# A graph-convolution and expert kernel: edge rows, statistics and the first projection in another order at the start

## The chip, the cores and the metric

The kernel runs on one core of a Trainium2 chip. The metric is the device time of one execution in microseconds (us), the median of three runs. One further execution was taken with the hardware profiler; its own time stands beside its span below. Engines: PE is TensorE, DVE VectorE, ACT ScalarE, POOL GpSimd, SP SyncE.

## The reference, cut to what matters

Two layers on 625 rows of 1024 features: a relational graph convolution with 20,000 edges and two relations, and a layer of eight experts (two taken per row) with two shared ones. The change touches the start of the first layer only:

```python
h      = layernorm(x)                            # 625 x 1024
norm_x = ln_weight * h * rsqrt(mean(h*h) + 1e-6)
out    = norm_x @ W_root + bias                  # 1024 -> 286
for r in range(2):
    w    = (edge_type == r)
    msg  = norm_x[src] @ W_rel[r] * w[:, None]
    sums = segment_sum(msg, dst, 625)
    cnt  = segment_sum(w, dst, 625)
    out  = out + sums / maximum(cnt, 1)[:, None]
x = x + h + elu(out) @ wo
x = x + experts(layernorm(x))
```

The edges come sorted by dst.

## The kernel before, in words

The 625 rows are five tiles of 125, called row 0 to row 4 here. The graph layer is done without gathers. The kernel counts, for each pair (source row, destination and relation), how many edges there are, and multiplies the projected rows with these counts.

**Loads (L520 to L552).** SP issues edge types, sources, x's row 0, the root weights, x's rows 1, then 2 and 3 in one load, row 4, and both relation weights (`load_x`, `load_w`), in this order; ACT issues the destinations and the layer-norm weights. POOL issues the bias (`cb`, L610), small vectors and the router's weights on a queue of its own.

**Edge columns (`edge_columns`, L664).** The three edge lists arrive as rows of 250. DVE turns them into float rows (L667 to L672), PE transposes them (L677), and ACT and DVE make three columns of them (L687 to L695): the source's position within its tile, a value that names the tile as a power of 16, and the destination key.

**Statistics (`stats`, L753).** For a row: two `bn_stats` on DVE, one for each half of 512, the aggregate, the negated mean (L760), and h = x - mean on ACT (L765). `scales` (L771) makes the factors of both norms from the variance.

**To columns (`to_columns`, L789).** PE transposes h in two groups of four blocks (L795); ACT evicts the first group in four instructions that multiply by the weights (L801), DVE the second in one (L798).

**Counts (`count_windows`, L828).** The edges are taken in 160 columns of 125, in groups of 4 (four groups) and then 8 (eighteen groups). For a group, DVE makes a one-hot of the sources (L849), multiplies it by the tile's value (L850), and a one-hot of the destination keys (L852). PE then does one count for each column (L868; two where a window crosses an accumulator's end).

**Projections (`project`, L886).** Projection i is eight steps of PE for one row and one weight matrix (L891): the first five are the root weights on rows 0 to 4, then the relations. Each step shows as two matmuls in the profile, about 0.51 us together.

**Order.** Below the loop stands an order written by hand: `at(c, f, ...)` runs f after the count of column c (L987 to L1021). A scheduler that knows estimated durations then orders each engine's instructions; `tc.issue_after(x)` keeps an instruction behind x on its engine, and each engine works in its order. Before the loop stand warm-up matmuls (`warm`, L970), the edge columns and the statistics of row 0; the first projection follows the count of column 7.

Of the kernel before, what the change touches and what calls it, by code (L numbers as in the profile page):

```python
# [18 lines left out]
D = 1024  # L19
E = 20000  # L20
R = 2
# [4 lines left out]
TP = 125  # L26
NT = N // TP
KD = D // 128
EP = 125
EC = E // EP  # L30
# [8 lines left out]
SPAN = (EP - 1 + 2 * SLACK) // DEG + 2  # L39
GROUPS = (4,) * 4 + (8,) * 18  # L40
# [412 lines left out]
def sparse_kernel(  # L453
# [24 lines left out]
    nc = tc.nc  # L478
# [33 lines left out]
    fbig = pool(front, "fbig", side="right")  # L512
    oneh = pool(front, "oneh", 8, side="right")
# [28 lines left out]
    def load_w(r, w):  # L542
        nc.sync.dma_start(wg[:, :, r, :], w.rearrange("(k p) f -> p k f", p=128))

    load_x(0, 1)
    load_w(R, W_root)
    load_x(1, 1)
    load_x(2, 2)
    for r in PARTS:
# [114 lines left out]
    def edge_columns():  # L664
        rowf = fbig.tile([EH, 2, 2 * EP], F32, name="rowf")
        two = [EH, 2, EP]
        nc.vector.tensor_tensor(rowf[:, 0].rearrange("c (j p) -> c j p", j=2),  # L667
                                rows_i["ety"].rearrange("c (j p) -> c j p", j=2),
                                low[:, 1][:, :, None].to_broadcast(two), op=ALU.subtract)
        nc.vector.scalar_tensor_tensor(rowf[:, 1], rows_i["dst"], float(R), rowf[:, 0],  # L670
                                       op0=ALU.mult, op1=ALU.add)
        nc.vector.tensor_copy(rowf[:, 0], rows_i["src"])  # L672
        p = ps_mm("p_edge")
        pv = p[:EP, : 2 * EC].rearrange("p (a j c) -> p a j c", a=2, j=2)
        for a in (0, 1):
            for j in range(2):
                nc.tensor.transpose(pv[:, a, j, :], rowf[:, a, j * EP : (j + 1) * EP], ident[:EH, :EH])  # L677
        wide = [EP, EH, 2, 2]

        def column(v):  # L680
            return v.rearrange("p (c j) b -> p c j b", j=2)

        def pairs(v):
            return v.rearrange("p j c -> p c j")[:, :, :, None].to_broadcast(wide)

        with tc.issue_after(table.ins):
            nc.scalar.copy(column(cols[:, KW_]), pairs(pv[:, 1]))  # L687

        q = fbig.tile([EP, 3, 2, EH], F32, name="q")
        nc.vector.tensor_scalar(q[:, 0], pv[:, 0], -float(TP // 2), 1.0 / TP, op0=ALU.add, op1=ALU.mult)  # L690
        nc.vector.tensor_scalar(q[:, 1], q[:, 0], ROUND, -ROUND, op0=ALU.add, op1=ALU.add)
        nc.vector.scalar_tensor_tensor(q[:, 2], q[:, 1], -float(TP), pv[:, 0], op0=ALU.mult, op1=ALU.add)
        nc.scalar.copy(column(cols[:, SP_]), pairs(q[:, 2]))

        return nc.vector.tensor_scalar(column(cols[:, VV_].bitcast(I16)), pairs(q[:, 1]), 4096.0, 7168.0,  # L695
                                       op0=ALU.mult, op1=ALU.add)


    flagf = const.tile([1, 2], F32, name="flagf")
# [53 lines left out]
    def stats(t):  # L753
        st = small.tile([TP, 2, 6], F32, tag="st", name=f"st_{t}")
        for s in range(2):
            with tc.issue_after((second[0] if t > 1 else evicted[1] if t else behind).ins):
                nc.vector.bn_stats(st[:, s, :], xh[:TP, t, s * 512 : (s + 1) * 512])
        nc.vector.bn_aggr(mv[:, t, :], st.rearrange("p a b -> p (a b)"))
        neg = small.tile([TP, 1], F32, tag="neg", name=f"neg_{t}")
        last = nc.vector.tensor_scalar(neg, mv[:, t, 0:1], -1.0, None, op0=ALU.mult)  # L760
        h = rows.tile([TP, D], F32, tag="h", name=f"h_{t}")
        with ExitStack() as order:
            if t == 1:
                order.enter_context(tc.issue_after(evicted[0].ins))
            moved = nc.scalar.activation(h, xh[:TP, t, :], AF.Identity, bias=neg)  # L765
        if t == 1:
            second.extend((last, moved))
        hs[t] = h
        return last
# [55 lines left out]
    MAXG = max(GROUPS)  # L825
    ends = [R * TP * min(DB * (b + 1), NT) for b in range((NT + DB - 1) // DB)]

    def count_windows(between):  # L828
        accs = []
        c0 = 0  # L830
        for g in GROUPS:
            oh_s = oneh.tile([EP, MAXG, 128], F16, tag="oh_s", name=f"ohs_{c0}")
            oh_k = oneh.tile([EP, MAXG, KR], F16, tag="oh_k", name=f"ohk_{c0}")

            def both(what, n):
                return [EP, g, n // 2, 2], cols[:, what, c0 : c0 + g][:, :, None, :].to_broadcast([EP, g, n // 2, 2])

            def halves(v):
                return v.rearrange("p g (a b) -> p g a b", b=2)

            order = ExitStack()
            if c0 == 0:
                order.enter_context(tc.issue_after(ahead.ins))
            elif c0 == 8:
                order.enter_context(tc.issue_after(second[0].ins))
            row = iota[:EP].rearrange("p (a b) -> p a b", b=2)
            shape, key = both(SP_, 128)
            os = halves(oh_s[:, :g, :])
            nc.vector.tensor_tensor(os, row[:, None].to_broadcast(shape), key, op=ALU.is_equal)  # L849
            nc.vector.tensor_tensor(os, os, both(VV_, 128)[1], op=ALU.mult)  # L850
            shape, key = both(KW_, KR)
            nc.vector.tensor_tensor(halves(oh_k[:, :g, :]), row[:, None, :SPAN].to_broadcast(shape), key,  # L852
                                    op=ALU.is_equal)
            order.close()
            for i in range(g):
                c = c0 + i
                a, z = R * LOW[c], R * min(LOW[c] + SPAN, N)
                for b, end in enumerate(ends):
                    base = ends[b - 1] if b else 0
                    f, t = max(a, base), min(z, end)  # L860
                    if f >= t:
                        continue
                    first = b == len(accs)
                    if first:
                        accs.append(psum[0].tile([128, 512], F32, tag="cnt", name=f"cnt_{b}", bufs=2))
                        nc.tensor.matmul(accs[b], nil[:, :128], nil, start=True, stop=False)
                    last = c == EC - 1 or R * LOW[c + 1] >= end
                    nc.tensor.matmul(accs[b][:, f - base : t - base], oh_s[:, i, :], oh_k[:, i, f - a : t - a],  # L868
                                     start=False, stop=last)
# [100 lines left out]
    def warm(n):  # L970
        for _ in range(n):
            nc.tensor.matmul(scrap[:, :128], iota, iota, start=True, stop=True)  # L972

    scrap = ps_acc("scrap")
    warm(24)
    behind = edge_columns()
    transpose_lnw()
    warm(40)
    ahead = stats(0)


# [541 lines left out]
```

## Time and profile before

| what | us |
|---|---|
| median of 3 runs | 304.88 (304.16 to 305.06) |
| profiled execution | 303.7 |
| its span | 301.4 |
| row 0's statistics begin on DVE | 7.68 |
| first count on PE | 10.30 |
| first transposes of x | 10.62 |
| first projection | 11.81 |
| last one-hot begins on DVE | 71.53 |
| end of the counts on PE | 73.08 |

A line of the timeline has the start, the busy time, the engine, the source line, the operation, what is written and read, the shape and the number of instructions merged. The chain of waits is followed back from the end; a piece of it has start, duration and what ran. In the parts with 40 characters, each is a fortieth of the span (7.5 us), in tenths of busy time.

### The profile page before, as it was taken

To read this page: it belongs to the slowest core of one execution; us is meant where nothing else is said; L and a number is where in the kernel's file an instruction comes from. 1 tells how busy PE (TensorE), PEld (TensorE's weight loads), DVE (VectorE), ACT (ScalarE), POOL (GpSimd) and SP (SyncE) were. 2 spreads that over 40 slices of the span, in tenths; PEclk is the share of its full clock that TensorE was granted. 3 is DMA by queue.
4 is the path that set the end of the run, shared out by engine and by line. 5 is a ranking of instruction groups with operands and counts; after the bars stand their busy time and mean duration, and the time that the engine had idled before them with its cause. 6 is when DMAs were issued, how large, how long until landed. Compare 5 with 4: busy or idle time off the path is not lost.

```text
span 301.4 us, 4682 instructions
## 1 busy us (share of the span) xinstructions
PE 290.8 (96%) x1649; PEld 194.9 (65%) x1649; DVE 168.4 (56%) x465; ACT 107.5 (36%) x246; POOL 45.2 (15%) x98
## 2 busy tenths in 40 slices
PE   8799999999999799999999999999999999999993
PEld 6687777787889534376777887887843334444452
DVE  5999999998327668756883122212223211255921
ACT  2455118355334432155123244638359311000000
POOL 9500000000000014240131212210003222200000
PEclk9999999999999999999999999999999999999998
DMA  7999910000009999965999253340057555479442
GB/s 243 304 318 393 421 65 2 0 2 1 0 17 340 348 348 391 400 195 182 348 396 410 86 203 96 114 141 3 0 190 276 221 209 210 191 291 385 161 138 73
DMA packets 27408, 61.15 MB, mean 203 GB/s; under 512 B 2176, under 2 KB 16007, under 8 KB 27375
## 3 DMA queue, kind: packets, MB, share of 16 engines
q1 hardware_dynamic: 21806, 43.77, 40.7%
q0 software_dynamic: 5280, 16.69, 15.7%
q10 hardware_dynamic: 294, 0.35, 0.5%
q8 instruction: 15, 0.25, 0.3%
q14 instruction: 13, 0.10, 0.1%
HBM read 42.76 MB, written 18.81 MB: 204 GB/s over the span
## 4 chain that ended last, share of the span: by engine, by line
PE 93%; DVE 4%; ACT 1%; issue 0%; ACTq 0%
PE p_pr L891 20%; PE p_h L1359 13%; PE p_yj L1417 13%; PE p_o L1472 11%; PE p_sh L1137 10%; PE p_y L952 6%; PE p_agg L909 6%; PE p_x L1340 3%; PE p_t L795 3%; PE cnt L868 2%; PE p_y L956 2%; PE p_hT L1371 1%; PE scrap L972 1%; PE p_gate L1085 1%; PE p_o L1474 1%; DVE ln_4s L727 0%
## 5 line engine op out<-in xcount | busy, mean ns | idle before, releaser
L891 PE MATMUL p_pr<-wg,nT 128*125 128x286 f32 x240 | 62.5, 409 | 0.0
L891 PEld LDWEIGHTS p_pr<-wg,nT 128*125 128x125 f32 x240 | 43.2, 187 | 11.3 <-ACT nT L801 0.2
L1359 PE MATMUL p_h<-w1a,xsT 128*128 (+2 forms) x176 | 40.0, 380 | 0.0
L1417 PE MATMUL p_yj<-w2a,hjT 128*128 (+2 forms) x88 | 38.6, 594 | 0.0
L1472 PE MATMUL p_o<-sw,shT 128*125 128x512 f32 (+1 forms) x88 | 36.1, 553 | 0.0
L1137 PE MATMUL p_sh<-h2T,sw 128*128 128x313 f32 (+1 forms) x128 | 35.2, 428 | 0.0
L1359 PEld LDWEIGHTS p_h<-w1a,xsT 128*128 128x128 f32 (+2 forms) x176 | 28.7, 168 | 7.4 <-issue 0.5
L1137 PEld LDWEIGHTS p_sh<-h2T,sw 128*128 128x128 f32 x128 | 23.6, 189 | 8.6 <-issue 0.2
L1417 PEld LDWEIGHTS p_yj<-w2a,hjT 128*128 128x128 f32 (+2 forms) x88 | 14.4, 168 | 22.4 <-issue 22.4
L1472 PEld LDWEIGHTS p_o<-sw,shT 128*125 128x125 f32 x88 | 16.4, 187 | 16.9 <-issue 16.2
L1421 DVE COPY ys<-p_yj 128x512 f32<-128x512 f32 x15 | 10.4, 692 | 28.7 <-PE p_yj L1417 26.5
L1363 DVE COPY hj<-p_h 128x256 f32<-128x256 f32 x11 | 4.7, 425 | 30.8 <-PE p_h L1359 30.8
L909 PE MATMUL p_agg<-P,CT 125*125 125x287 bf16 x150 | 20.1, 287 | 1.6 <-DVE agg L915 1.6
L966 POOL DMA_DIRECT2D x1d<-xh x10 | 5.3, 532 | 98.5 <-DVE xh L959 98.5
L909 PEld LDWEIGHTS <-CT 125*125 125x125 bf16 x150 | 18.5, 136 | 2.5 <-issue 2.0
L1425 POOL DMA_INDIRECT yt<-ys,row x11 | 10.8, 984 | 50.5 <-DVE ys L1421 50.5
L952 PE MATMUL p_y<-wo_t,eT 128*125 128x512 f32 x40 | 18.1, 595 | 0.0
L1332 POOL DMA_INDIRECT xs<-h2d,tok x11 | 11.2, 1015 | 45.0 <-PE p_x L1340 30.9
L1374 ACT ACTIVATE hjT<-p_hT,vT 128x128 f32<-128x128 f32 (+2 forms) x34 | 8.7, 332 | 24.5 <-PE p_hT L1371 24.5
L1344 DVE COPY xsT<-p_x 128x512 f32<-128x512 f32 x11 | 7.6, 692 | 17.4 <-PE p_x L1340 13.8
L1448 DVE SCALAR_TENSOR_TENSOR x<-p_o,x 125x512 f32<-125x512 f32 (+1 forms) x11 | 6.9, 641 | 16.3 <-PE p_o L1474 16.3
L1359 PE MATMUL p_h<-w1m,xsT 128*64 128x256 f32 (+1 forms) x96 | 14.7, 381 | 0.0
(302 smaller groups left out, 424.0 us busy)
## 6 DMA issues: line engine op xcount, KB each, us to landing
w1a<-in_L_ffn_W_dram SPq DMA_DIRECT2D x8, 1024.0 KB, 10.5
w2a<-in_L_ffn_W_dram SPq DMA_DIRECT2D x8, 1024.0 KB, 4.8
yt<-zero SPq DMA_DIRECT2D x2, 2560.0 KB
g<-yt SPq DMA_DIRECT2D x10, 512.0 KB, 6.7
sw<-in_L_ffn_sW_dram SPq DMA_DIRECT2D x4, 1024.0 KB, 5.0
x<-x1d SPq DMA_DIRECT2D x5, 500.0 KB
wg<-in_L_gnn_W_rel_dram SPq DMA_DIRECT2D x2, 1144.0 KB, 19.1
x1d<-xh POOLq DMA_DIRECT2D x5, 448.0 KB, 6.7
```

The lines of the kernel that those rows point to most:

```text
L795: nc.tensor.transpose(pv[:, k, :], row[:, at : at + 128], ident[:TP, :TP])
L891: nc.tensor.matmul(p[:TP, :F], nT[:, k, m * TP : (m + 1) * TP], wg[:, k, r, :], start=(k == 0), stop=(k == KD - 1))
L909: nc.tensor.matmul(p[:TP, : F + 1], CT[:, m, at : at + TP], P[:, m, r, i], start=(m == 0 and i == 0), stop=(m == NT - 1 and i == 2))
L952: nc.tensor.matmul(ps[s][:TP, :], eT[:, k, :], wo_t[:, k, s * 512 : (s + 1) * 512], start=(k == 0), stop=False)
L1137: nc.tensor.matmul(p[:, : z - a], sw1[:, i, k, t * 128 : (t + 1) * 128], h2T[:, k, a:z], start=(k == 0), stop=(k == KD - 1))
L1332: nc.gpsimd.indirect_dma_start(out=xs, out_offset=None, in_=h2d, in_offset=bass.IndirectOffsetOnAxis(ap=tok[:, j : j + 1], axis=0))
L1340: nc.tensor.transpose(p[:, k * 128 : (k + 1) * 128], xs[:, at : at + 128], ident)
L1359: nc.tensor.matmul(p[a:b, :H], xsT[j][:, k, a:b], w1m[j, a][:, 0, k, :] if a else w1a[:, bass.ds(e, 1), k, :], start=(k == 0), stop=(k == ...
L1417: made = nc.tensor.matmul(p[a:b], hjT[:, j, k, a:b], w2m[j, a, k][:, at] if a else w2a[:, bass.ds(e, 1), k, at], start=(k == 0), stop=(k = ...
L1421: nc.vector.tensor_copy(y[:, at], p)
L1425: sent.append(nc.gpsimd.indirect_dma_start(out=yt, out_offset=bass.IndirectOffsetOnAxis(ap=row[:, j : j + 1], axis=0), in_=y, in_offset=No ...
L1472: nc.tensor.matmul(p[:TP, :n], shT[:, i, k, own], sw2[:, i, k, at], start=(i == 0 and k == 0), stop=False)
```

## The change

- x's row 0 is loaded in two halves of 512 columns, and the root weights in two loads of four blocks each.
- In `edge_columns` the two transposes go to two PSUM tiles; the part that makes the source columns becomes `source_columns` and runs on DVE behind row 0's statistics. The position's column is written by DVE directly, where ACT copied it before (L693).
- h of rows 0 and 1 is made half by ACT and half by DVE.
- Row 0's transposes and the first projection are put ahead of all counts; the first group of one-hots is made behind row 0's eviction, and row 1's statistics behind these.
- Warm-up matmuls: 18 and 24 where there were 24 and 40.
- The hand-written places of statistics, transposes, scales and projections among the counts are moved.

```diff
-    load_x(0, 1)
-    load_w(R, W_root)
+    HALVES = [slice(s * 512, (s + 1) * 512) for s in range(2)]
+    for s in HALVES:
+        nc.sync.dma_start(xh[:, 0, s], x[:128, s])
+    load_w(R, W_root, slice(0, KD // 2), slice(KD // 2, KD))
     load_x(1, 1)
...
-        p = ps_mm("p_edge")
...
+        ps = [ps_acc("p_edge"), ps_mm("p_edge_k")]
...
+            nc.scalar.copy(cols[:, KW_], pairs(ps[1][:EP, :EC]))
+        return got, ps[0][:EP, :EC]
...
+    def source_columns(v, behind):
...
+        with tc.issue_after(behind.ins):
+            nc.vector.tensor_scalar(q[:, 0], v, -float(TP // 2), 1.0 / TP, op0=ALU.add, op1=ALU.mult)
         nc.vector.tensor_scalar(q[:, 1], q[:, 0], ROUND, -ROUND, op0=ALU.add, op1=ALU.add)
-        nc.vector.scalar_tensor_tensor(q[:, 2], q[:, 1], -float(TP), pv[:, 0], op0=ALU.mult, op1=ALU.add)
-        nc.scalar.copy(column(cols[:, SP_]), pairs(q[:, 2]))
+        nc.vector.scalar_tensor_tensor(cols[:, SP_], pairs(q[:, 1]), -float(TP), pairs(v),
                                        op0=ALU.mult, op1=ALU.add)
...
-            with tc.issue_after((second[0] if t > 1 else evicted[1] if t else behind).ins):
+            with tc.issue_after((second[0] if t > 1 else first if t else behind).ins):
                 nc.vector.bn_stats(st[:, s, :], xh[:TP, t, s * 512 : (s + 1) * 512])
...
+        own, rest = (HALVES[0], HALVES[1]) if t < 2 else (slice(0, D), None)
...
-            moved = nc.scalar.activation(h, xh[:TP, t, :], AF.Identity, bias=neg)
+            moved = nc.scalar.activation(h[:, own], xh[:TP, t, own], AF.Identity, bias=neg)
+        if rest:
+            with tc.issue_after(last.ins):
+                last = nc.vector.tensor_scalar(h[:, rest], xh[:TP, t, rest], neg, None, op0=ALU.add)
...
+    def one_hots(c0, g):
...
+            if c0 < 8:
+                order.enter_context(tc.issue_after((second[0] if c0 else evicted[1]).ins))
...
-    warm(24)
-    behind = edge_columns()
-    transpose_lnw()
-    warm(40)
-    ahead = stats(0)
+    warm(18)
+    behind, sources = edge_columns()
+    transpose_lnw()
+    warm(24)
+    source_columns(sources, stats(0))
+    to_columns(0, hs[0], nT, True)
...
-    for t, (c0, c1) in enumerate(((0, 3), (4, 9), (13, 19), (16, 22), (20, 26))):
+    for t, (c0, c1) in enumerate(((0, 3), (6, 11), (9, 14), (13, 18))):
         if t:
-            at(c0, stats, t)
-        at(c1, to_columns, t, None, nT, True)
+            at(c0, stats, t + 1)
+        at(c1, to_columns, t + 1, None, nT, True)
...
-    at(6, scales, 0, 2)
-    at(18, scales, 2, 4)
-    at(21, scales, 4, NT)
-    for i, c in enumerate((7, 15, 21, 24, 28, 46, 64, 82, 100, 118, 134, 148)):
-        at(c, project, i)
+    at(10, scales, 2, 4)
+    at(14, scales, 4, NT)
+    for i, c in enumerate((3, 12, 15, 20, 38, 56, 74, 92, 110, 128, 146)):
+        at(c, project, i + 1)
...
+    oh_s, oh_k, first = one_hots(0, GROUPS[0])
+    made[0] = oh_s, oh_k
+    stats(1)
+    scales(0, 2)
+    project(0)
     count_windows(between)
```

Bodies that only moved into a function of their own (the three one-hot instructions, now L853, L854 and L857) are left out above.

More of the change, by code (lines that the diff above doesn't have):

```diff
@@ L540, in load_x, with load_w @@
                                                        ap=[[D, 128], [TP * D, n], [1, D]]))
-    def load_w(r, w):
-        nc.sync.dma_start(wg[:, :, r, :], w.rearrange("(k p) f -> p k f", p=128))
-    load_x(0, 1)
-    load_w(R, W_root)
+    def load_w(r, w, *ks):
+        for k in ks or (slice(0, KD),):
+            nc.sync.dma_start(wg[:, k, r, :], w.rearrange("(k p) f -> p k f", p=128)[:, k])
+    HALVES = [slice(s * 512, (s + 1) * 512) for s in range(2)]
+    for s in HALVES:
+        nc.sync.dma_start(xh[:, 0, s], x[:128, s])
+    load_w(R, W_root, slice(0, KD // 2), slice(KD // 2, KD))
     load_x(1, 1)
@@ L671, in edge_columns, with pairs @@
                                        op0=ALU.mult, op1=ALU.add)
-        nc.vector.tensor_copy(rowf[:, 0], rows_i["src"])
-        p = ps_mm("p_edge")
-        pv = p[:EP, : 2 * EC].rearrange("p (a j c) -> p a j c", a=2, j=2)
+        got = nc.vector.tensor_copy(rowf[:, 0], rows_i["src"])
+        ps = [ps_acc("p_edge"), ps_mm("p_edge_k")]
         for a in (0, 1):
             for j in range(2):
[L677 to L684, printed above, removed]
-        with tc.issue_after(table.ins):
-            nc.scalar.copy(column(cols[:, KW_]), pairs(pv[:, 1]))
-        q = fbig.tile([EP, 3, 2, EH], F32, name="q")
-        nc.vector.tensor_scalar(q[:, 0], pv[:, 0], -float(TP // 2), 1.0 / TP, op0=ALU.add, op1=ALU.mult)
+                nc.tensor.transpose(ps[a][:EP, j:EC:2], rowf[:, a, j * EP : (j + 1) * EP], ident[:EH, :EH])
+        with tc.issue_after(table.ins):
+            nc.scalar.copy(cols[:, KW_], pairs(ps[1][:EP, :EC]))
+        return got, ps[0][:EP, :EC]
+    def pairs(v):
+        return v[:, :, None].to_broadcast([EP, EC, 2])
+    def source_columns(v, behind):
+        q = fbig.tile([EP, 2, EC], F32, name="q")
+        with tc.issue_after(behind.ins):
+            nc.vector.tensor_scalar(q[:, 0], v, -float(TP // 2), 1.0 / TP, op0=ALU.add, op1=ALU.mult)
         nc.vector.tensor_scalar(q[:, 1], q[:, 0], ROUND, -ROUND, op0=ALU.add, op1=ALU.add)
-        nc.vector.scalar_tensor_tensor(q[:, 2], q[:, 1], -float(TP), pv[:, 0], op0=ALU.mult, op1=ALU.add)
-        nc.scalar.copy(column(cols[:, SP_]), pairs(q[:, 2]))
-        return nc.vector.tensor_scalar(column(cols[:, VV_].bitcast(I16)), pairs(q[:, 1]), 4096.0, 7168.0,
+        nc.vector.scalar_tensor_tensor(cols[:, SP_], pairs(q[:, 1]), -float(TP), pairs(v),
                                        op0=ALU.mult, op1=ALU.add)
+        nc.vector.tensor_scalar(cols[:, VV_].bitcast(I16), pairs(q[:, 1]), 4096.0, 7168.0,
+                                op0=ALU.mult, op1=ALU.add)
     flagf = const.tile([1, 2], F32, name="flagf")
@@ L826, in sparse_kernel, with both, halves @@
     ends = [R * TP * min(DB * (b + 1), NT) for b in range((NT + DB - 1) // DB)]
+    made = {}
+    def one_hots(c0, g):
+        oh_s = oneh.tile([EP, MAXG, 128], F16, tag="oh_s", name=f"ohs_{c0}")
+        oh_k = oneh.tile([EP, MAXG, KR], F16, tag="oh_k", name=f"ohk_{c0}")
+        def both(what, n):
+            return [EP, g, n // 2, 2], cols[:, what, c0 : c0 + g][:, :, None, :].to_broadcast([EP, g, n // 2, 2])
+        def halves(v):
+            return v.rearrange("p g (a b) -> p g a b", b=2)
+        row = iota[:EP].rearrange("p (a b) -> p a b", b=2)
+        shape, key = both(SP_, 128)
+        os = halves(oh_s[:, :g, :])
+        with ExitStack() as order:
+            if c0 < 8:
+                order.enter_context(tc.issue_after((second[0] if c0 else evicted[1]).ins))
+            nc.vector.tensor_tensor(os, row[:, None].to_broadcast(shape), key, op=ALU.is_equal)
+        last = nc.vector.tensor_tensor(os, os, both(VV_, 128)[1], op=ALU.mult)
+        shape, key = both(KW_, KR)
+        with tc.issue_after(last.ins):
+            nc.vector.tensor_tensor(halves(oh_k[:, :g, :]), row[:, None, :SPAN].to_broadcast(shape), key,
+                                    op=ALU.is_equal)
+        return oh_s, oh_k, last
     def count_windows(between):
@@ L831, in count_windows @@
         for g in GROUPS:
[L832 to L854, printed above, removed]
+            oh_s, oh_k = made.pop(c0) if c0 in made else one_hots(c0, g)[:2]
             for i in range(g):
```

## The prediction

> **What bounds the kernel now.** I read the page first, then the chain of waits, the busy times by stretch, the timelines of VectorE (DVE) and TensorE (PE), and the DMA view by the microsecond. The page:
>
> ```profile
> span 301.4 us, 4682 instructions
> ...
> PE 290.8 (96%) x1649; PEld 194.9 (65%) x1649; DVE 168.4 (56%) x465; ACT 107.5 (36%) x246; POOL 45.2 (15%) x98
> ...
> PE   8799999999999799999999999999999999999993
> ...
> DVE  5999999998327668756883122212223211255921
> ```
>
> PE is busy in all slices but the first few. DVE's 56% is an average: its first nine slices (to about 68 us) are full too. The chain of waits over the first 45 us, trimmed:
>
> ```profile
> 7.76 1.21 DVE st L757 x2
> ...
> 10.62 1.07 PE p_t L795 x8
> 11.70 0.11 PE cnt L868 x4
> 11.81 4.10 PE p_pr L891 x16
> ...
> 15.97 0.89 PE p_t L795 x8
> ...
> 17.03 3.98 PE p_pr L891 x16
> ...
> 37.29 3.94 PE p_pr L891 x16
> ```
>
> Until 10.3 us PE does only warm-up and edge transposes; from 11.81 (first projection) it never stops. By stretch (columns: busy PE, PEld, DVE, ACT, POOL, clock, DMA share, GB/s):
>
> ```profile
> 4.20:6.60 2.40, 2.40 (x22) 2.23 (x20) 0.05 (x2) 0.49 (x2) 2.40 (x6) 1.00 1.04 371
> ...
> 12.30:28.00 15.70, 15.70 (x91) 12.30 (x91) 15.57 (x59) 8.65 (x21) 1.95 (x8) 1.00 1.06 343
> ...
> 50.00:72.20 22.20, 22.16 (x169) 17.44 (x167) 22.13 (x46) 11.02 (x32) 0.00 (x0) 1.00 0.00 1
> 72.20:100.00 27.80, 26.41 (x174) 23.07 (x172) 13.64 (x44) 12.08 (x36) 0.00 (x0) 1.00 0.38 122
> ```
>
> From 12.3 to 72.2 us DVE is as full as PE, and the DMA engines are full at the start. DVE's idle 2.4 us at 4.2 is what the change wants to use. DVE's timeline, row 1's and row 2's statistics and the last one-hot:
>
> ```profile
> 12.33 1.28 DVE L757 BATCH_NORM_STATS2 st<-xh 125x6 f32<-125x512 f32 x2
> ...
> 15.75 0.67 DVE L757 BATCH_NORM_STATS2 st<-xh 125x6 f32<-125x512 f32 x1
> ...
> 71.53 0.68 DVE L850 TENSOR_TENSOR ohs<-ohs,cols 125x1024 f16<-125x1024 f16 x1
> ```
>
> The last one-hot is ready at 72.21; PE counts with it at 72.88 (11 counts from 72.78, the last 8 with it). So DVE has 0.67 us of slack at the end of the counts. The DMA view from 7 to 8 us, a line for each queue (packets, MB, share of 16 engines):
>
> ```profile
> q0 software_dynamic: 19, 0.09, 93.2%
> q1 hardware_dynamic: 151, 0.17, 48.2%
> ```
>
> GpSimd's bias load (L610) holds the engines with 19 packets; from 8 to 9 us only 81 GB/s move. The trace also records each load's 16 landings. The last ones: x's row 0 at 5.74, root weights 10.68, row 1 at 11.91, rows 2 and 3 (one load) at 15.01. In the kernel before none is waited for: DVE asks for row 1 at 12.33 and row 2 at 15.75.
>
> [...] row 1's 16 landings spread from 10.99 to 11.91. [...] The trace: 24 warm-ups in 2.68 us (112 ns), later 40 in 2.41 (60 ns). [...] The trace: L731 takes 0.81 us for 1024 elements, L783 1.28.
>
> **The change part by part.** *Loads.* Row 0 and the root weights become two loads each: two more issues on SP of 0.42 us (row of the first x load), so row 1's issue moves from 2.59 to about 3.4, rows 2 and 3, row 4 and the relation weights behind it by as much. Their bytes wait behind the root weights anyway (row 1's packets start after 9 us): cost 0; without that cover 0.84. In the built program loads reuse eight completion counters, so row 1's issue waits for dst's landing (3.10): over by then. The GpSimd queue is not touched, so bias packets and bytes ahead of rows 1 to 3 stay as they are. I therefore keep 10.68, 11.91 and 15.01, with bounds of 1.5 us earlier (should the bias burst fall elsewhere) and 0.8 later.
>
> *Row 0.* Its first half lands between 4.6 and 5.74 (take 4.65), the second between 5.74 and 6.2 (5.85). DVE: second half's statistics 5.85, then +0.71 aggregate, +0.25 negated mean, +0.17 (the steps from 8.28 to 9.39 before): 6.98. New on DVE: half of h, no row in the trace. Bounds from L731: 0.41 (half of 0.81) and 0.68 (L757's rate); I take 0.54, 0.45 to the next start. The source columns follow: 0.36, 0.28, 0.40, 0.24, to 8.71. One of ScalarE's (ACT) copies (L693, 0.46) goes. ACT's half of h: 1.15 for 1024 now, so between 0.57 and 1.15; take 0.72, to 7.70. Transposes at 7.75, first projection 1.19 later (10.62 to 11.81 before): **8.94 instead of 11.81**. Its fifth step wants the second weight half at 10.99, which landed at 10.68: no wait. It ends at 13.04. The 22 warm-ups dropped cost or win nothing (idle PE).
>
> *Row 1: the new wait.* DVE evicts at 8.87 (0.59), makes the first one-hots (0.45+0.34+0.19) to 10.44, and then waits for row 1 until 11.95: 1.5 us, in order, with every later one-hot and statistic behind it. It adds 1.31+0.25+0.17: 13.68; ACT's half: 14.40; row 1's transposes 14.45 (15.97 before). PE idles from 13.2 to 14.45.
>
> *Row 2: the second wait.* DVE: half of h (0.45), a one-hot (0.33), 14.46; rows 2 and 3 at 15.01. Row 2's statistics start at 15.05, against 15.75. All that was added on DVE ahead of this (two halves of h, 0.9; a wider column) hides in these two waits; without them it costs 1.0.
>
> *DVE from there.* It is 0.70 earlier, but three groups of one-hots, less one instruction, are still to be made: three times 0.86 (0.33+0.19+0.34) less 0.33, 2.25. It is 1.55 late. From 15.75 to 72.21 are 56.46 us of the same work, 0.47 of it waits: last one-hot at 15.05+2.25+56.46 = 73.76, or 73.29 without the waits.
>
> *PE from there.* The built order feeds row by row. Row 2's mean after 3.75 us of DVE work (18.8), ACT's root and h to 20.15, transposes 20.2. Row 3's mean 2.65 later (21.3), ACT behind two evictions, h to 22.85. Row 4's mean at 26.15, h to 27.55. The fourth projection starts at 28.0 (27.29 before, one count more done), the sixth at about 37.5 (37.29) with equally many counts done. So **the 2.87 us won at the first projection are gone: 0.2 late**. Until 72 us the built order moves counts behind later projections: the last counts stand behind one more step of 0.51. PE reaches them at 72.88+0.51+0.2 = 73.6; the one-hot is there between 73.3 and 73.8: another 0 to 0.2. After them PE has work queued and DVE is slack.
>
> Sum: +0.2 and +0.1 = +0.3 us. The profiled execution took 303.7 (span 301.4 and 2.3 around it); after it 304.0. The median of the runs is 1.2 above the profiled one: 304.88 becomes **305.2**.
>
> **Rivals.** *The early start goes through:* rows 1 to 3 land before they are asked for, because the bias burst comes at another moment or the smaller packets spread better. DVE then wins both waits, 2.1 us: 305.2-2.1 = 303.1. For it: the burst is a matter of GpSimd's timing. Against: nothing in its queue changes, and the bytes ahead are the same. *Slower: the counts wait for DVE.* The place is the last group of one-hots. Everything beyond 73.6 goes one to one into the end. If rows 2 and 3 land 0.8 later (the SP issues show after all), the one-hot is ready at about 74.4: +0.8 to +1.1, 306.0. For it: DVE without slack; against: the queue's backlog. *The change does not do what it says:* the order follows the built program, so only the landing of row 0 could fail; up to 1.5 us there are covered by the wait for row 1, and the time is that of the forecast.
>
> **How the numbers follow.** A measurement tells about 0.3% (0.9 us) from no change. Forecast 0.61, 304.4 to 305.8 of its own: no change. Early start goes through 0.24 (302.5 to 303.9): faster. Counts wait 0.15 (305.9 to 306.6): slower. The range goes down to 302.9, leaving out about 0.07 of the first rival, and up to 305.9, leaving out about 0.13.
>
> **What would show it.** Right: first projection near 8.9; DVE idle for a DMA of x ahead of L759 near 10.4 to 12, and again near 15; PE idle near 13 to 14.5; sixth projection near 37.5; last one-hot near 73.5 and DVE full to there. Wrong: row 1 landed by 10.5 (then PE does not idle at 13), or PE waiting for one-hots around 73.

## The result, and the profile after

The changed kernel takes 306.76 us (median of 9 runs, 305.75 to 307.58), against 304.88 for the kernel before: 1.0053 of its time, 95% interval 1.0033 to 1.0073. That is slower by half a per cent, clear of the noise, and above the range of the prediction, which ended at 305.9. The time around the span is 1.8 to 2.0 us in the executions of the changed kernel and 2.2 to 2.4 in those of the kernel before, so by spans the distance is larger: 304.9 against 302.6 us (medians; that of the kernel before is of its 37 executions beside the runs e). The profiled execution took 307.44 us with a span of 305.5; of the 4.1 us between the two spans, 3.0 are there when PE begins its last matmul, and 1.1 come after it, while the output is stored. That last stretch took 5.5 us in the trace of before, 6.6 here and 5.6 in a second trace of the same kernel, so it is not the change.

The page of the changed kernel:

```profile
span 305.5 us, 4643 instructions
...
PE 292.2 (96%) x1627; PEld 194.7 (64%) x1627; DVE 169.5 (55%) x467; ACT 106.6 (35%) x245; POOL 45.1 (15%) x98
...
PE   8889999999999799999999999999999999999991
...
DVE  6689999999525758765884122212223212256920
```

Where the kernel before has 879 and 599 at the start of these two rows, there is now 888 and 668: PE does more in its second slice, but both engines have a third slice that isn't full, and DVE a second one. DVE's full stretch is longer in return (a 9 and a 5 in the tenth and eleventh slice, 8 and 3 before). DVE's timeline in the second and third slice and at the last one-hots shows why; brackets hold the idle time ahead of an instruction and what ended it:

```profile
13.47 1.29 DVE L759 BATCH_NORM_STATS2 st<-xh 125x6 f32<-125x512 f32 x2 [1.64 <-DMA xh<-in_x_dram]
...
15.23 0.49 DVE L772 TENSOR_SCALAR h<-xh,neg 125x512 f32<-125x512 f32 x1
15.63 0.42 DVE L853 TENSOR_TENSOR ohs<-iota,cols 125x512 f16<-125x512 f16 x1
17.44 0.69 DVE L759 BATCH_NORM_STATS2 st<-xh 125x6 f32<-125x512 f32 x1 [1.39 <-DMA xh<-in_x_dram]
...
75.91 0.39 DVE L857 TENSOR_TENSOR ohk<-iota,cols 125x464 f16<-125x464 f16 x1
```

DVE waits for row 1 to 13.47 and for row 2 to 17.44. Its last one-hot is ready at 76.30, where the kernel before had it at 72.21. PE's timeline:

```profile
9.82 2.19 PE L902 MATMUL p_pr<-wg,nT 128*125 128x286 f32 x8
...
14.25 0.28 PE L879 MATMUL cnt<-ohk,ohs 125*128 125x58 f16 x4
16.00 1.08 PE L802 MATMUL p_t<-ident,h 125*128 125x125 f32 x8 [1.47 <-ACT h L769]
...
22.47 1.07 PE L802 MATMUL p_t<-ident,h 125*128 125x125 f32 x8 [0.56 <-ACT h L769]
...
29.79 0.54 PE L802 MATMUL p_t<-ident,h 125*128 125x125 f32 x3 [0.53 <-ACT h L769]
```

The first projection starts 2 us earlier than before (9.82 against 11.81), and PE gives it all back waiting for centred rows. The last matmul, first before and then after:

```profile
295.95 0.27 PE L1474 MATMUL p_o<-b,wT 96*125 96x256 bf16 x1
```

```profile
298.94 0.27 PE L1490 MATMUL p_o<-b,wT 96*125 96x256 bf16 x1
```

### The profile page after: what moved, and what is told of

It is laid out like the page before. It is cut to its first block, busy times and chain, and to the rows that moved or that the text cites. A ratio compares the mean times of both kernels' runs of the same rounds, so it can differ in the third digit from the quotient of the medians.

```text
span 305.5 us, 4643 instructions
## 1 busy us (share of the span) xinstructions
PE 292.2 (96%) x1627; PEld 194.7 (64%) x1627; DVE 169.5 (55%) x467; ACT 106.6 (35%) x245; POOL 45.1 (15%) x98
## 4 chain that ended last, share of the span: by engine, by line
PE 85%; DVE 6%; DMA 4%; SPq 1%; ACT 1%; issue 1%; ACTq 0%
PE p_pr L902 16%; PE p_h L1375 13%; PE p_yj L1433 13%; PE p_o L1488 11%; PE p_sh L1153 10%; PE p_y L963 6%; PE p_agg L920 6%; DMA xh<-in_x_dram 4%; PE p_x L1356 3%; PE p_y L967 2%; PE cnt L879 2%; PE p_t L802 1%; DVE st L759 1%; PE p_hT L1387 1%; PE p_gate L1101 1%; PE p_o L1490 1%
## 5 line engine op out<-in xcount | busy, mean ns | idle before, releaser
L902 PE MATMUL p_pr<-wg,nT 128*125 128x286 f32 x240 | 64.1, 411 | 0.7 <-DMA wg<-in_L_gnn_W_root_dram 0.2
## 6 DMA issues: line engine op xcount, KB each, us to landing
wg<-in_L_gnn_W_rel_dram SPq DMA_DIRECT2D x2, 1144.0 KB, 20.2
```

Source lines behind the costliest of these rows:

```text
L902: nc.tensor.matmul(p[:TP, :F], nT[:, k, m * TP : (m + 1) * TP], wg[:, k, r, :], start=(k == 0), stop=(k == KD - 1))
```

## The experiments

Two stages of the loss can be told apart: the loads land late, and DVE and PE are held by them. Theory A: late rows hold DVE, and DVE's last one-hot holds PE one to one. Theory B: GpSimd's burst of bias packets makes the landings late. Theory A': the split loads make them late. Rivals: PE's slow start, with 1.7 us for row 0's transposes where the kernel before took 1.07 (C), DVE's added work (D), a stray trace (E), and the later issue of the rows on SP, since two more loads stand ahead of them.

All 18 runs, with the last of a load's 16 landings (us, of the trace; "2+3" is row 2 alone where rows 2 and 3 are separate loads), the end of the last one-hot and the start of the last matmul on PE. The median of the kernel before was 304.87, 304.96, 304.49, 304.66 and 304.37 beside the runs e, f, g, h and i. The ratio is against it.

| run | what | median | ratio (95%) | row 1 | rows 2+3 | last one-hot | last matmul |
|---|---|---|---|---|---|---|---|
| before | | 304.88 | | 11.90 | 15.01 | 72.21 | 295.95 |
| after | | 306.76 | 1.0053 (1.0033 to 1.0073) | 13.45 | 17.41 | 76.30 | 298.94 |
| e1 | whole loads | 306.48 | 1.0069 (1.0042 to 1.0095) | 12.28 | 16.11 | 74.98 | 297.63 |
| e2 | before, loads split | 305.41 | 1.0007 (0.9982 to 1.0032) | 13.16 | 17.44 | 73.83 | 297.59 |
| e3 | bias late, added by GpSimd | 307.08 | 1.0081 (1.0053 to 1.0109) | 11.02 | 13.96 | 74.07 | 296.72 |
| e4 | more warm-ups | 306.24 | 1.0038 (1.0019 to 1.0057) | 12.79 | 16.19 | 75.08 | 297.74 |
| f1 | one-hots in the waits | 305.09 | 1.0006 (0.9985 to 1.0027) | 13.16 | 17.48 | 73.89 | 297.24 |
| f2 | no bias | 305.87 | 1.0022 (0.9999 to 1.0045) | 12.33 | 16.08 | 74.95 | 297.60 |
| f4 | h on ACT alone | 306.98 | 1.0068 (1.0041 to 1.0095) | 13.03 | 16.75 | 75.51 | 298.17 |
| f5 | row 1 first | 305.73 | 1.0029 (1.0012 to 1.0046) | 7.71 | 14.08 | 73.85 | 296.50 |
| g1 | f1 and f5 | 304.32 | 1.0006 (0.9984 to 1.0028) | 7.32 | 13.59 | 72.60 | 295.95 |
| g2 | g1, h on ACT alone | 306.78 | 1.0071 (1.0049 to 1.0093) | 8.54 | 13.98 | 72.12 | 295.72 |
| g3 | after again | 306.41 | 1.0049 (1.0028 to 1.0070) | 13.31 | 17.32 | 76.20 | 298.86 |
| g4 | before, no bias | 304.96 | 1.0010 (0.9994 to 1.0027) | 10.58 | 13.79 | 72.23 | 295.98 |
| h1 | bias on SP's queue | 305.84 | 1.0029 (1.0008 to 1.0049) | 11.37 | 17.73 | 76.61 | 299.25 |
| h2 | h1 and f1 | 304.04 | 0.9987 (0.9969 to 1.0005) | 11.79 | 15.62 | 72.52 | 295.87 |
| h3 | h2, h on ACT alone | 306.55 | 1.0054 (1.0032 to 1.0077) | 11.94 | 17.95 | 74.40 | 298.01 |
| h4 | h1 with whole loads | 303.98 | 0.9981 (0.9965 to 0.9997) | 11.10 | 15.23 | 74.10 | 296.75 |
| i1 | h1, copies late | 305.37 | 1.0026 (1.0010 to 1.0042) | 12.14 | 16.44 | 75.32 | 297.97 |
| i2 | all cures | 304.09 | 0.9985 (0.9968 to 1.0002) | 10.95 | 14.41 | 73.10 | 296.45 |

The last four columns are one execution each, a median is of 6 to 22; where they disagree (e1, e3, g2), the text says what is known. The ratios are of times, with the time around the span in them. Its median was 2.1 to 2.3 us in before, e1, f2, g4, h1 to h4, i1 and i2, and 1.8 to 2.0 in the others; what sets it isn't known.

Two distances can be read from the table. From the last landing of rows 2 and 3 to the end of the last one-hot there are 58.87 to 58.89 us in the changed kernel, e1, e4, f2, g3, h1, h4 and i1, though the landing moves by 2.5 us between them (15.23 to 17.73): in these eight the landing sets all that follows. From there to the start of the last matmul there are 222.64 to 222.66 us in these and in e3, f4 and f5, and 223.35 with the order of f1 (f1, g1, h2, i2). This second distance does not show that PE waits for the last one-hot. In e1, e4, f2, g3, h1, h4 and i1 PE's fourth projection (30.17 us in the changed kernel) has already moved by as much as the last matmul, to 0.02 us: what sets these runs apart is complete by 30 us, and from there both engines run in step.

### Do the late rows cost the time?

**g3, the changed kernel once more.**

> The changed kernel once more, unchanged, for a second trace of its landings on the chip of the other runs. Theory A: row 1 lands at 12.5 to 13.5, rows 2 and 3 at 16.0 to 17.5, DVE waits for both, last one-hot near 75 to 76.3, time 306.3 to 307.0. Rival E (the first trace was a stray one): rows 2 and 3 land near 15.0 and the last one-hot is near 73.8.

Median 306.41. The last landings of rows 1 to 3, the last one-hot and the last matmul repeat to 0.15 us. Three more traces with the same loads and the burst have rows 2 and 3 at 16.19 (e4), 16.75 (f4) and 17.48 (f1), all later than 15.01. E falls: the late landings are the kernel's own, though their size varies.

**f1, the same loads, but work for DVE in its waits.** In `stats`, in the function that makes one-hots, and where both are called:

```diff
-            with tc.issue_after((second[0] if t > 1 else first if t else behind).ins):
+            with tc.issue_after((third if t > 1 else first if t else behind).ins):
...
-            if c0 < 8:
-                order.enter_context(tc.issue_after((second[0] if c0 else evicted[1]).ins))
+            if c0 < 12:
+                order.enter_context(tc.issue_after((second[0] if c0 > 4 else first if c0 else evicted[1]).ins))
...
     made[0] = oh_s, oh_k
+    *made[4], first = one_hots(4, GROUPS[1])
     stats(1)
+    *made[8], third = one_hots(8, GROUPS[2])
```

> The changed kernel with the loads and all work as they are, but the second group of one-hots made on DVE ahead of row 1's statistics and the third ahead of row 2's, so that DVE has work while it waits for x. Theory A (late rows hold up DVE, and DVE's last one-hot holds up PE one to one): DVE's idle 1.64 and 1.39 us ahead of these statistics shrink to under 0.5 each, the last one-hot is ready near 73.8 to 74.3 instead of 76.3, the last count as much earlier, time 304.3 to 305.2. Rival (PE's own start, or the landings themselves, set the end): no gain, 306.2 to 307.2.

```profile
11.48 0.27 DVE L857 TENSOR_TENSOR ohk<-iota,cols 125x232 f16<-125x232 f16 x1
13.18 1.29 DVE L759 BATCH_NORM_STATS2 st<-xh 125x6 f32<-125x512 f32 x2 [1.44 <-DMA xh<-in_x_dram]
...
17.50 0.70 DVE L759 BATCH_NORM_STATS2 st<-xh 125x6 f32<-125x512 f32 x1 [0.59 <-DMA xh<-in_x_dram]
...
73.51 0.38 DVE L857 TENSOR_TENSOR ohk<-iota,cols 125x464 f16<-125x464 f16 x1
```

Rows 1, 2 and 3 land as late as in the changed kernel (the statistics start at 13.18 and 17.50), but the second group of one-hots is done by 11.75, the third before row 2. The last one-hot is ready 2.4 us earlier (73.89), the last matmul starts 1.7 earlier, and the median is 305.09: 1.7 us of the 1.9 are back, by DVE's order alone. PE has the gain early: its sixth projection starts at 38.10 us, 39.50 in the changed kernel, with the same matmuls done. The waits were expected under 0.5 us; the second shrank to 0.59, and the first stayed at 1.44, since DVE was also earlier by nearly a microsecond (PE's transposes of row 0 took 1.1 instead of 1.7; PE then lost this start to a wait of 1.21 us for the second weight half). So the late rows cost time through DVE's waits: the first half of A stands, and the rival (the time is set elsewhere) falls. That PE is held by the last one-hot of all, A's second half, is not shown.

**g4, the kernel before without the bias**, which its result lacks. The control: landings earlier, where nobody waits for them.

> The kernel before with the convolution bias left out, neither loaded nor added. The weights and rows 1 to 3 should land 1 to 2 us earlier (near 9.5, 10.7 and 13.5). Theory A: DVE never waits for x in this kernel, so nothing later moves: 304.5 to 305.3. Rival F (early landings win time by another way than DVE's waits): 304.0 or less.

Rows 2 and 3 land 1.2 us earlier, the last one-hot at 72.23 and the last matmul at 295.98 are as before to 0.03 us, and the time is 304.96. Here an earlier landing is worth nothing, as no engine asks for the row by then.

### What makes them late?

**e1, whole loads again** (its edit is below), and **e2, the kernel before with split loads** (the reverse edit in that kernel):

```diff
-    for s in HALVES:
-        nc.sync.dma_start(xh[:, 0, s], x[:128, s])
-    load_w(R, W_root, slice(0, KD // 2), slice(KD // 2, KD))
+    load_x(0, 1)
+    load_w(R, W_root)
```

> The changed kernel with row 0 of x and the root weights loaded whole again (two loads instead of four). Theory A (the split loads themselves made rows 1 to 3 land late, and late rows pin DVE and DVE pins PE): row 1 lands near 12.0 us and rows 2 and 3 near 15.0, as in the kernel before; row 2's statistics start near 15.1, the last one-hot is ready near 73.8, time 304.5 to 305.5. Rival B (the split is innocent: GpSimd's bias burst or plain variation did it): landings stay near 13.4 and 17.4, last one-hot near 76, time 306.3 to 307.0. Row 0's statistics start 0.3 to 0.7 us later in both, which the wait for row 1 covers.

> The kernel before with only its first two loads split in halves; all else as it was. Theory A: rows 1 to 3 land near 13.4 and 17.4, DVE, which asks for row 1 at 12.3 and for row 2 at 15.75, waits 1.1 us and then about 0.6 more, the last one-hot is ready near 73.9 instead of 72.2, and of these 1.7 us the 0.67 of slack hides a part: 305.7 to 306.2. Rival B: landings stay at 11.9 and 15.0 and the time at 304.6 to 305.2.

In the traces both go with A': in e1 the last landings are 1.2 and 1.3 us earlier than in the changed kernel and the last matmul 1.3; in e2 they are 1.3 and 2.4 later than before and the last matmul 1.6. The times don't follow as clearly: e1's median is 306.48, not told apart from the changed kernel's, and e2's ratio is not told apart from 1. A part of this is the time around the span: 2.3 us in e1, where the changed kernel has 1.9, and 1.9 in e2, where the kernel before has 2.3. By spans e1 is 0.7 us under the changed kernel (304.2 against 304.9), and e2 0.9 over the kernel before (303.5 against 302.6). Nor is e1's edit free: PE waits 1.58 us for the whole weights ahead of its first projection.

e2's expectation let a slack of 0.67 us hide a part of DVE's delay. It hid nothing: PE was 1.65 us late at row 3's transposes already (25.42 for 23.78), and the last one-hot (1.63) and the last matmul (1.64) were late by as much.

**e3, f2, the bias late or left out.** In e3 the five root projections leave the bias out (not shown) and GpSimd adds it later; f2 has neither the load nor the additions, and its result lacks the bias:

```diff
-    nc.gpsimd.dma_start(cb, bcast_rows(conv_bias, TP))
...
     at(50, clear)
+    at(50, lambda: nc.gpsimd.dma_start(cb, bcast_rows(conv_bias, TP)))
+    for t in range(NT):
+        at(100, lambda t=t: nc.gpsimd.tensor_add(agg[:, t, :], agg[:, t, :], cb))
```

> The changed kernel with GpSimd's load of the convolution bias moved from the start to after the fiftieth chunk of counts; the five root projections then leave the bias out and GpSimd adds it at the hundredth chunk. Theory B (the burst of bias packets holds the shared DMA engines): the weights' second half, row 1 and rows 2 and 3 land 1 to 2.4 us earlier than in the changed kernel (near 10.7, 12.0 and 15.5), the last one-hot is ready near 74, time 304.3 to 305.3. Theory A: the landings gain no more than the bias's own 0.4 us of bytes, time 306.2 to 306.8.

> The changed kernel with the convolution bias left out altogether: it is neither loaded nor added, all else is as it was. Theory B (the burst of bias packets is what makes the landings late): second weight half near 9.7, row 1 near 11.0, rows 2 and 3 near 14.0, last one-hot near 74, and now without anything added later the time is 304.3 to 305.3. Rival: the landings come early again but the time stays at 306.5 to 307.1, as the median with the late bias did; then the landings of these rows do not set the time.

The landings came forward by 2.4 and 3.5 us in e3, by 1.1 and 1.3 in f2, but e3's median is 307.08. e3 didn't do what I meant: GpSimd ran its additions as soon as it could, at 21 to 38 us, in the middle of DVE's full stretch. DVE's timeline there (e3):

```profile
30.21 0.76 DVE L722 SCALAR_TENSOR_TENSOR ln_4o<-ln 125x1 f32<-125x1 f32 x1
...
37.74 0.99 DVE L856 TENSOR_TENSOR ohk<-iota,cols 125x464 f16<-125x464 f16 x1
```

and GpSimd's:

```profile
29.99 0.96 POOL L1013 TENSOR_TENSOR agg<-agg,cb 125x286 f32<-125x286 f32 x1 [7.50 <-DVE ln L720]
...
37.31 1.17 POOL L1013 TENSOR_TENSOR agg<-agg,cb 125x286 f32<-125x286 f32 x1 [3.21 <-DVE agg L911]
```

In the changed kernel these DVE instructions take 0.15 and 0.40. From row 0's statistics to the last one-hot DVE is busy for 67.3 us in e3 and for 65.9 in the changed kernel: 1.4 us more; these two alone are longer by 0.61 and 0.59. Of GpSimd's additions the two beside them took 0.96 and 1.17 us; another, at 33.41, took 0.69, and the DVE instruction beside it took its usual 0.67 (L804). PE felt it: its sixth projection was 2.8 us earlier than in the changed kernel, its last matmul 2.2. But this loss is in a trace of the fastest of e3's eight executions (304.91), so it does not explain the median of 307.08, which stays open: e3 says nothing of the time that earlier rows win. Its landings stand, and they settle one rival: rows 2 and 3 were issued at 4.56 us, as in the changed kernel (4.66; 3.21 before), and had landed by 13.96, so the later issue on SP is not what made them late.

**h1, h4, the bias on SP's queue**, behind rows 2 and 3, with nothing to add later; h4 has the whole loads too:

```diff
     load_x(2, 2)
+    nc.sync.dma_start(cb, bcast_rows(conv_bias, TP))
...
-    nc.gpsimd.dma_start(cb, bcast_rows(conv_bias, TP))
```

> The changed kernel with the convolution bias loaded on SyncE's queue behind rows 2 and 3 instead of on GpSimd's at the start; nothing else is moved. Theory B (the burst of bias packets makes the landings late): second weight half near 9.7, row 1 near 11.0, rows 2 and 3 near 14.0, last one-hot near 74, time 304.6 to 305.3. Theory A' (the split loads do it, through one late engine): rows 2 and 3 still land at 16 or later, last one-hot near 75, time 305.5 to 306.7.

> The changed kernel with whole loads of row 0 and the root weights, and the bias on SyncE's queue. Theory B: weights near 9.4, row 1 near 10.5, rows 2 and 3 near 13.7, about as with split loads and the bias moved; time 304.6 to 305.3. Theory A' (the split makes an engine late): rows 2 and 3 land at least 1.5 us earlier here than with the split loads and the bias moved, and the time is at least 1 us lower than there.

The DMA view from 8 to 10 us, of the changed kernel:

```profile
DMA packets 205, 0.31 MB, mean 156 GB/s; under 512 B 40, under 2 KB 165, under 8 KB 205
q0 software_dynamic: 69, 0.12, 47.9%
q1 hardware_dynamic: 136, 0.20, 33.3%
```

and of h1:

```profile
DMA packets 398, 0.74 MB, mean 370 GB/s; under 512 B 101, under 2 KB 258, under 8 KB 398
q1 hardware_dynamic: 300, 0.73, 100.6%
```

With the burst less than half as much moves: 31 bias packets took 663 ns each on the mean, 20.6 us of engine time or 1.3 us of all sixteen engines; without them the rate is 370 GB/s, not 156. Yet h1 is at 305.84 and its last landing of rows 2 and 3 at 17.73. The sixteen landings of that load show two different things (first, median, last):

| | before | e2 | after | e1 | h1 | i1 | h4 | i2 |
|---|---|---|---|---|---|---|---|---|
| loads | whole | split | split | whole | split | split | whole | whole |
| bias burst | yes | yes | yes | yes | no | no | no | no |
| first | 13.57 | 13.41 | 13.71 | 13.24 | 12.50 | 12.81 | 12.59 | 12.71 |
| median | 13.92 | 14.91 | 15.05 | 14.68 | 13.07 | 13.65 | 13.18 | 13.62 |
| last | 15.01 | 17.44 | 17.41 | 16.11 | 17.73 | 16.44 | 15.23 | 14.41 |

The burst moves the median (15.05 to 13.07 between the changed kernel and h1). The split moves the last landing: over all twelve traces with split loads in this order it comes 0.8 to 4.7 us after the median, 2.4 to 2.5 in the middle, and over the five with whole loads 0.8 to 2.1, 1.1 in the middle. The two groups overlap: in e4 and e3, both split, it is 0.8 and 0.9. A wait ends with the last: in the changed kernel row 2's statistics start at 17.44, the last landing is at 17.41.

The times of h1 and h4, run side by side, differ by 1.9 us (305.84 and 303.98), and those of e1 and h4 by 2.5. So each cure, whole loads or the bias moved, is clear of the noise once the other is in; alone, neither is (306.48 and 305.84, against 306.76). In this sense A' and B are both right.

**i1, the other burst.** In h1 GpSimd no longer waits for the bias (3.12 us ahead of the first copy in the changed kernel), so its copies of the expert biases, with packets of 32 KB that take 1.2 to 1.4 us, start at 13.0 us instead of 17.0, beside rows 2 and 3. i1 puts them on SP's queue behind the output weights.

> The changed kernel with the bias on SyncE's queue behind rows 2 and 3, and the copies of the expert biases (packets of 8 and 32 KB) on SyncE's queue behind the output weights. If those copies made the stray landings of the run with the bias alone moved: rows 2 and 3 land evenly, first near 12.5 and last under 14.5, row 2's statistics start near 14, last one-hot near 73.9, time 304.0 to 304.8 with a narrow spread. If the split loads did: the last landing is still at 15.5 to 17.7 and the time near 305.8.

It missed: 305.37, last landing 16.44. The trace shows one landing of sixteen late already at the first half of the weights (8.98, the others by 7.56), then at the second (10.99, by 9.51), at row 1 (12.14, by 10.98) and at rows 2 and 3 (16.44, by 14.73). f2 has the same single late landings (11.28, the others by 9.24; 16.08, by 13.41); e3, also split, hasn't. At the first half of the weights one landing is over 0.7 us behind the rest in six of the twelve traces. With whole weights without the burst (h4, i2, g4) the last landing is within 0.7 us of the one before it at the weights and at row 1; at rows 2 and 3 it is 1.1 behind in h4 and 0.4 in i2 and g4. Why one landing falls behind with split loads, in half of the executions, and whether it is the same DMA engine's each time, is not known.

### The rivals

**e4, more warm-ups** (24 and 28 for 18 and 24).

> The changed kernel with 24 and 28 warm-up matmuls instead of 18 and 24. The row-0 transposes should take near 1.1 us instead of 1.7 and the first projection start near 9.2 instead of 9.8. Theory (late rows pin DVE, DVE pins PE): nothing after the wait for row 1 moves, last one-hot near 76, time 306.3 to 307.2. Rival C (the cold start of PE sets the end): the end comes 0.6 us earlier, 306.2 or less, with PE early at the second projection too.

Row 0's transposes took 1.0 us instead of 1.7, and the first projection started at 9.53 instead of 9.82, having waited 0.26 us for weights; 306.24 is not told apart from the changed kernel's 306.41 to 306.76. Its last one-hot and its last matmul came 1.2 us earlier, as much as its rows 2 and 3 landed earlier. C is not what sets the end.

**f4, rows 0 and 1 centred on ACT alone.**

```diff
-        own, rest = (HALVES[0], HALVES[1]) if t < 2 else (slice(0, D), None)
+        own, rest = slice(0, D), None
```

> The changed kernel with rows 0 and 1 centred wholly on ScalarE again, as before the change; the two half rows on DVE (0.49 us each) are gone. Theory A: the 0.98 us were hidden in DVE's two waits for x, so row 2's statistics still start near 16 to 17.5 with its landing, row 1's transposes 0.4 later, time 306.3 to 307.0. Rival D (the work added on DVE is what costs): the last one-hot comes 0.9 us earlier against row 2's landing, time 305.6 to 306.0.

306.98: nothing won. From row 2's landing to the last one-hot there are 58.76 us, 0.12 less than in the changed kernel, where D wants 0.9. D falls; the 0.98 us on DVE were hidden in its waits, as the prediction had it. PE also lost time to a lower clock in this trace (0.50 for 3.4 us, told at the end); it had made that up by the fourth projection (29.40, 30.17 in the changed kernel).

### Followed to its end

**f5**, row 1 ahead of the root weights and rows 2 and 3 as two loads; **g1**, that with f1's order; **g2**, g1 with ACT alone.

```diff
+    load_x(1, 1)
     load_w(R, W_root, slice(0, KD // 2), slice(KD // 2, KD))
-    load_x(1, 1)
-    load_x(2, 2)
+    load_x(2, 1)
+    load_x(3, 1)
```

> The changed kernel with x's row 1 loaded ahead of the root weights, and rows 2 and 3 as two loads. Same bytes. Theory A: row 1 lands near 8 us, before DVE asks for it (no wait there), the second weight half near 13.4 (PE then waits for it within the first projection), row 2 near 15.5 and row 3 near 17.4; row 2's statistics start 1.5 to 2 us earlier than in the changed kernel, last one-hot near 74.4, time 304.8 to 305.4. Rival C (PE's start sets the end): the first projection now ends later and the time is 306.5 or more.

> The changed kernel with both cures at once: one-hots of the second and third group in DVE's waits, and row 1 of x loaded ahead of the root weights, rows 2 and 3 as two loads. Theory A: DVE no longer waits for x after its first statistics; from 5.4 us it has some 66.3 us of work and a few tenths of small waits, so the last one-hot is ready near 72.5; PE, which starts its first projection near 9.2 to 11.1, is then the later of the two and reaches its last counts near 73.3: time 304.0 to 304.7, level with the kernel before or a little under it. Rival C: PE's wait for the second weight half (1.8 us with this order) costs what DVE wins, 305.1 or more.

> As the run with both cures, and rows 0 and 1 centred wholly on ScalarE. DVE loses 0.98 us of work that no wait covers any more. Theory A: if DVE's last one-hot is still what the last counts wait for, it comes 0.9 us earlier and the time falls by 0.3 to 0.9 against that run; if PE is the later of the two there, the time stays within 0.3 of it. In the changed kernel itself the same edit gained nothing (306.98).

f5 won 1.0 us where 1.4 to 2.0 were expected, with PE waiting 1.8 us for the second weight half. g1 came out as expected, 304.32: no wait for x but the first, last one-hot at 72.60, last matmul at 295.95 as in the kernel before. g2 missed: its traced last matmul is 0.23 us earlier, but the median is 306.78. The clock granted over a run had a median of 0.993, against 0.995 for g1; in g2's trace PE is idle for 2.30 us at the first projection, and its clock stays at full there. The cause stays open.

**h2**, h1 with f1's order; **h3**, that with ACT alone; **i2**, whole loads, bias and copies late, f1's order.

> As the run before, and the one-hots of the second and third group in DVE's waits for x. No wait for x is left but the first; DVE's 66.4 us of work from 5.4 us with half a us of small waits end at 72.3 to 72.8, the last counts follow 0.45 later, as in the run with fill alone: time 303.8 to 304.5, level with the kernel before or just under it. If PE's path of its own were the later: last counts wait for no one-hot.

> As that, with rows 0 and 1 centred on ScalarE alone. Theory A: DVE is shorter by 0.98 us, now uncovered, so the last one-hot comes near 71.5, the last counts near 72.1, and the time falls by 0.5 to 0.9 against that run, 303.0 to 303.8, 0.3 to 0.5% under the kernel before. Rival C: PE is late by 0.4 at the first projection, cannot follow, and gains nothing[...].

> Whole loads of row 0 and the root weights, bias and copies late on SyncE's queue, and the one-hots of groups two and three in DVE's waits; what stays of the change is the order (row 0 and the first projection ahead of all counts, two half rows centred on DVE). No wait for x but the first. DVE's 66 us of work from 5.8 us end near 72.5, the last counts follow 0.45 later near 72.9: time 303.4 to 304.2, 0.2 to 0.4% under the kernel before. Rival C: PE waits for the whole root weights (near 9.5) and its end gains nothing, 304.5 or more.

h2 304.04 and i2 304.09 as expected, h3 missed (306.55; in its trace rows 2 and 3 landed at 17.95, with DVE waiting 2.85 us for them). The best is h4, 303.98, ratio 0.9981 (0.9965 to 0.9997). Its DVE:

```profile
11.97 1.28 DVE L758 BATCH_NORM_STATS2 st<-xh 125x6 f32<-125x512 f32 x2
...
15.25 0.69 DVE L758 BATCH_NORM_STATS2 st<-xh 125x6 f32<-125x512 f32 x1 [0.72 <-DMA xh<-in_x_dram]
...
73.71 0.39 DVE L856 TENSOR_TENSOR ohk<-iota,cols 125x464 f16<-125x464 f16 x1
```

One wait is gone and the other halved. So the new order itself loses nothing once its rows are there, and wins next to nothing: h2, h4 and i2 are within 0.2% of the kernel before.

## Why the prediction was wrong

| step | predicted | measured |
|---|---|---|
| row 0's halves landed | 4.65, 5.85 | 5.48, 6.18 |
| row 0's transposes | 7.75 | 8.26 |
| first projection | 8.94 | 9.82 |
| row 1's statistics | 11.95 | 13.47 |
| row 1's transposes | 14.45 | 16.00 |
| row 2's statistics | 15.05 | 17.44 |
| row 2's transposes | 20.2 | 22.47 |
| fourth projection | 28.0 | 30.17 |
| sixth projection | 37.5 | 39.50 |
| last one-hot ready | 73.3 to 73.8 | 76.30 |

**Right: both waits and the sum behind them.** Two waits of DVE for rows 1 and 2 and one of PE ahead of row 1's transposes came where they were foretold. From row 2's statistics to the last one-hot the prediction had 2.25 + 56.46 = 58.71 us; it took 58.86. DVE's added work was hidden, as said (f4). The slower rival named the cause, a late landing of rows 2 and 3 with a DVE that has no slack behind it; where it is paid, it had wrong.

**Wrong: "I therefore keep 10.68, 11.91 and 15.01, with bounds of 1.5 us earlier (should the bias burst fall elsewhere) and 0.8 later."** The changed kernel's landings were 12.11 for the second weight half, 13.45 and 17.41: 1.5 and 2.4 us later for the rows, far beyond the bound. Rows 1 and 2 set everything behind them, so 15.05 became 17.44 and 73.76 became 76.30.

PE's own path slipped with it. The forecast had the sixth projection at 37.5, with as many counts done as before; it came at 39.50 with eight counts fewer. When the twelfth projection starts, PE has done the same matmuls in both kernels, first before and then after:

```profile
68.56 1.21 PE L891 MATMUL p_pr<-wg,nT 128*125 128x286 f32 x4
```

```profile
71.39 3.62 PE L902 MATMUL p_pr<-wg,nT 128*125 128x286 f32 x14
```

It is 2.83 us late there, and 3.0 at the last matmul. The last groups of one-hots add only the difference, some 0.2 us. So the rival's picture, PE ready at 73.6 and then held one to one until 76.30, is not what happened; that these 2.7 and the forecast's 0.3 add up to the measured 3.0 is luck.

The argument for the landings ("their bytes wait behind the root weights anyway", "the bytes ahead are the same") put the cost of the split at 0: it priced a load by its bytes and its issue. The runs show that a wait ends with the last of sixteen landings (17.41 and 17.44 in the changed kernel), that these spread further with split loads (from first to last 4.03 us in e2 against 1.44 in the kernel before, 5.23 in h1 against 2.64 in h4; by what mechanism stays open), and that the bias burst lasted longer: the last of its 31 packets started at 8.76 us in the kernel before and at 9.14 in e1, with whole loads, at 10.12 here and between 9.3 and 10.6 in all others with split loads and the burst at the start. The sentence "nothing in its queue changes" was true and no reason: the packets of GpSimd's queue took 93.2% of the sixteen engines' time from 7 to 8 us in the kernel before and 34.9% here, and 36.2% from 8 to 10 us before and 47.9% here.

**Smaller misses.** Row 0 was 0.5 late at the transposes, and these took 1.7 us instead of 1.07. The warm-ups ahead of them were slow too: the 18 + 24 took 114 to 117 ns each, where the last 40 before took 60. The trace's record of the granted clock begins, at full, at 9.69 us here and at 6.22 before; ahead of that it has none. "The 22 warm-ups dropped cost or win nothing" was wrong by 0.6 us at the first projection in this trace, and the wait for row 1 covered it (e4). It differs between executions: in f1, with the same warm-ups, the last 24 took 90 ns each on the mean and the transposes 1.07 us. And the time around the span was 1.9 us, where 2.3 had been carried over: 0.4 us in the forecast's favour.

## What to carry to other kernels

A landing that nobody waits for has an unknown price (1.2 us earlier won nothing in g4): moving a consumer ahead can turn it into the bound, and then the last of its sixteen completions counts (17.41 us here, for statistics that started at 17.44). Look at what else the DMA engines carry at that moment (156 GB/s moved from 8 to 10 us in the changed kernel, with the bias burst, and 370 in h1, without it), and measure split loads against whole ones: here, with the bias moved, whole ones did better by 1.9 us (h4 and h1). Before advancing a consumer past its data, give the engine work to do in the wait: here two groups of one-hots put ahead of the statistics recovered 1.7 of 1.9 us. And an experiment that moves work to an idle engine must be read for what that engine then does to its neighbours: in e3 DVE was busy for 1.4 us more.

## What the runs showed of the hardware

**A stretch at half clock behind an idle time of PE of 2.07 us.** In f4 PE sat idle for that long ahead of row 1's transposes (they start at 16.01), and its granted clock was then 0.50 for 3.4 us. By stretch (busy PE, PEld, DVE, ACT, POOL, clock, DMA share, GB/s):

```profile
13.00:16.50 3.50, 1.43 (x13) 1.06 (x12) 1.98 (x5) 1.34 (x2) 2.03 (x8) 1.00 1.06 267
16.50:19.90 3.40, 3.40 (x12) 2.67 (x11) 3.12 (x12) 1.14 (x4) 0.00 (x0) 0.50 1.08 259
19.90:24.00 4.10, 3.95 (x31) 3.13 (x30) 4.10 (x23) 2.77 (x5) 0.00 (x0) 1.00 1.08 357
```

The eight transposes took 1.50 us there, 1.08 in the changed kernel. The changed kernel, idle for 1.47 us at the same place, kept its clock (1.00 in all three stretches), and so did f5 (idle for 1.83 us). Longer idle times left the clock alone: 2.30 us in g2, 2.60 in h1. The pages of before, after, f5, g1 and g2 show no fall of the clock in the first 39 of their 40 slices. So the length of the idle time alone doesn't tell these cases apart; what does is not shown.

**The last of sixteen.** In i1 fifteen landings of rows 2 and 3 lie within 1.9 us (12.81 to 14.73) and the sixteenth is 1.7 us later (16.44); the wait pays for the one: row 2's statistics start at 16.47, behind 1.73 us of waiting.
